# Cross-attention with token queries: moving one subtraction, writing out SyncE's order, and moving the output's 64 rows

## The chip, the cores and the metric

The kernel runs on one core of a Trainium2 chip. A core has five engines that run their own instruction queues and wait for each other through semaphores: TensorE (PE, matrix products, with its weight loads listed apart as PEld), VectorE (DVE), ScalarE (ACT), GpSimd (POOL), and SyncE (SP), which here only issues transfers (DMA). The metric is the time of one execution on the device in microseconds. Before the change: 973.11 us, the median of three runs (971.55 to 974.76).

## The reference

For each of 16 batches there are 100 query rows of width 640 and 718 encoder rows of width 384, with 4 more token rows behind them. Everything is fp32. Eight heads of width 80. Cut to what is computed:

```python
query = x @ Wq
hs = mha(query, enc @ Wk, enc @ Wv)          # over 718 encoder rows
ca_q1 = (ca^T @ Wq_ca)[:, indices]           # 100 rows out of 384, from the 4 token rows
ca_hs1 = mha(ca_q1, x, x)                    # over the 100 rows of x
ca_hs2 = mha(ca_hs1 @ Wq, ca @ Wk_ca, ca @ Wv_ca)   # over the 4 tokens
out = (hs + ca_hs2) @ Wout + b_out + x
```

## The kernel before

The encoder rows of a batch are taken as three thirds of 240 (width `KT`), each as two pieces of up to 120 keys (`KN`). V and most of K are computed with a scheme of 15 products in place of 18: sums and differences of blocks of the encoder (`enc_sums`, L466 to L485, on GpSimd, into the tile `enc`) are multiplied with sums and differences of weight blocks. A product adds into a running PSUM bank, named A to E in `V_PLAN` (L93) and `K_PLAN` (L111), and after each product the state of its bank is read out into the result: the first time by a ScalarE copy (L392), later by an addition on VectorE (L390). The next product into the same bank has to wait until the read is done. `vv.go(n)` does the next n products of V for batch b, `kk.go(n)` those of K for batch b + 1. A fifth chunk of the keys is computed plainly by `last_keys` (L543, copied out by ScalarE at L554).

The main loop goes over the batches (L1090). In a middle batch (the branch at L1183) TensorE does, in this order: the scores of batch b (L598), the small products of the second attention, the products of V for b and of K for b + 1 mixed, `last_keys`, the output projection of finished rows (`last.project`, L926), the queries of the next two batches in every second batch (L519), and the attention product of batch b (L1267, `a_ps`). VectorE meanwhile takes the maximum of the scores (`larger`, `Maximum`), and then three times `subtract` (L1112) takes it off one of three score tiles `st` of 120 x 1600; ScalarE's `exponential` (L1120) follows each. The attention product needs all three tiles.

The output has 1600 rows, cut into tiles `OC` (L33) of 128 rows, one of 64 rows and a last one of 128. A tile is projected in the iteration after the batch that completes it; in iterations 1, 5, 10 and 14 there is none. The 64 rows are completed in batch 14 and projected in the last iteration by `project_few` (L948): their two halves of 320 columns are put on the two halves of the partitions. `Last.load` (L872) brings the rows of `x` into `xn` and adds the bias on GpSimd (L883).

Orders: TensorE, VectorE, ScalarE and GpSimd follow the program's order from L1083 on (`tc.manual_schedule`). SyncE is not in that set, so its transfers are put in an order by a scheduler. They are: `xT` (L201), `enc` (L217), `rest` (L226), `mb` (L686), `ca` (L711), `xn` (L882), `out` (L942, L946, L965). A transfer at the head of SyncE's queue that waits for its buffer holds up all behind it. The tile `rest` holds two blocks of the encoder and has one buffer, read last by `last_keys` of its batch; `enc` has two buffers, read last by the products of V. `va_d` to `vb` is a transfer of 1000 KB that GpSimd issues itself (L802).

As the schedule puts them before the change, `mb` for two batches ahead stands in front of the `enc` and `rest` of the next-but-one batch.

Of the kernel before, what the change touches and what calls it, by code (L numbers as in the profile page):

```python
# [14 lines left out]
B, S, H = 16, 100, 640  # L15
# [17 lines left out]
OC = [(r, P) for r in range(0, B * S - P - 64, P)] + [(B * S - P - 64, 64), (B * S - P, P)]  # L33
# [91 lines left out]
def kernel(  # L125
# [33 lines left out]
    def pair(name):  # L159
        tile = ps2.tile([P, 2, 512], F32, tag="ps2", name=name)  # L160
        return tile
# [4 lines left out]
    def psumk(name):  # L166
        return psk.tile([P, 512], F32, tag="psk", name=name)
# [38 lines left out]
    def enc_tile(name):  # L206

        return inp.tile([P, NF, KT], F32, tag="enc", name=name)

    def rest_tile(name):  # L210
        return main.tile([P, len(A_REST), KT], F32, tag="rest", name=name)

    def load_enc(b):
        enc = enc_tile(f"enc_{b}"), None
        for u, lo, hi in ((0, 0, 3), (1, 1, 3), (2, 0, 2)):
            at = A_RAW[u, lo]
            nc.sync.dma_start(  # L217
                out=enc[0][:, at : at + hi - lo],
                in_=enct[b][:, lo:hi, u * (KT - 1) : u * (KT - 1) + KT],
            )  # L220
        return enc

    def load_rest(b, enc):
        rest = rest_tile(f"rest_{b}")
        for (u, c), i in A_REST.items():
            nc.sync.dma_start(  # L226
                out=rest[:, i], in_=enct[b][:, c, u * (KT - 1) : u * (KT - 1) + KT]
            )
        return enc[0], rest
# [634 lines left out]
    class Last:  # L864
# [51 lines left out]
        def project(self, chunks=range(HC)):  # L916
            for r, xn in self.xn.items():
                lo, n = OC[r]
                if n <= 64:
                    self.project_few(r, xn)  # L920
                    continue
                if chunks[0] == 0:
                    self.o_ps = pair(f"o_ps_{r}")
                o_ps = self.o_ps
                for c, k in [(c, k) for k in range(2) for c in chunks]:
                    nc.tensor.matmul(  # L926
                        o_ps[:n, k, : H // 2],
                        hsTs[r][:, c, :n],
                        wout_sb[:, c, k * (H // 2) : (k + 1) * (H // 2)],
                        start=(c == 0),  # L930
                        stop=(c == HC - 1),
                    )
                if chunks[-1] < HC - 1:
                    continue
                o_v = out.rearrange("b s n -> (b s) n")[lo : lo + n]
                if self.split:
                    for k in range(2):
                        cols = slice(k * (H // 2), (k + 1) * (H // 2))
                        nc.vector.tensor_tensor(
                            xn[:n, cols], o_ps[:n, k, : H // 2], xn[:n, cols], ALU.add  # L940
                        )
                        nc.sync.dma_start(out=o_v[:, cols], in_=xn[:n, cols])  # L942
                    continue
                both = xn[:n].rearrange("p (k d) -> p k d", k=2)
                nc.vector.tensor_tensor(both, o_ps[:n, :, : H // 2], both, ALU.add)
                nc.sync.dma_start(out=o_v, in_=xn[:n])  # L946

        def project_few(self, r, xn):  # L948
            lo, n = OC[r]
            o_ps = pair(f"o_ps_{r}")[:, 0]  # L950
            for c in range(HC):
                for at, cols in self.parts(n):
                    nc.tensor.matmul(
                        o_ps[at : at + n, : H // 2],
                        hsTs[r][:, c, :n],
                        wout_sb[:, c, cols],
                        start=(c == 0),
                        stop=(c == HC - 1),
                    )
            nc.vector.tensor_tensor(  # L960
                xn[:, : H // 2], o_ps[:, : H // 2], xn[:, : H // 2], ALU.add
            )
            o_v = out.rearrange("b s n -> (b s) n")[lo : lo + n]
            for at, cols in self.parts(n):
                nc.sync.dma_start(out=o_v[:, cols], in_=xn[at : at + n, : H // 2])  # L965
# [111 lines left out]
    for n in range(HC):  # L1077
# [4 lines left out]
    last, enc_next, second_next = None, load_rest(1, load_enc(1)), Second(1, xT)  # L1082
# [2 lines left out]
        mybir.EngineType.PE,  # L1085
        mybir.EngineType.DVE,
        mybir.EngineType.Activation,
    }
    ctx.enter_context(tc.manual_schedule(engines=engines))
    for b in range(B):  # L1090
# [5 lines left out]
        def loads():  # L1096

            if b == 0:
                nc.sync.dma_start(
                    out=wout_sb, in_=wout.rearrange("(c p) n -> p c n", p=P)  # L1100
                )
            if b + 2 >= B:
                return None, None, None
            x_next = xT_at[0] if b % 2 else load_x(p + 1)
            xT_at[0] = x_next
            return Second(b + 2, x_next), load_enc(b + 2), load_m(b + 2)
# [4 lines left out]
        def subtract(i):  # L1111
            return nc.vector.tensor_tensor(  # L1112
                st[i],
                st[i],
                top.over[:KN].unsqueeze(1).to_broadcast([KN, 2, ROWS]),
                ALU.subtract,
            )

        def exponential(i):
            nc.scalar.activation(st[i], st[i], AF.Exp, scale=SCALE)  # L1120
# [31 lines left out]
        if b + 1 < B:  # L1152
            kk = Keys(b + 1, enc)

        if b == 0:
            now.scores2()
            now.softmax3()
            second.scores1()
            top.go(3)
            kk.go(3)  # L1160
            top.go(1)
            first_values(3, e_in, (act, act), (0,), bank)
            kk.go(2)
            top.go()
            first_values(3, e_in, (act, act), (1,), bank)
            kk.go(3)
            first_values(0, e_in, (act, act), (0,), bank)
            kk.go(2)
            subtract(0)
            exponential(0)  # L1170
            first_values(0, e_in, (act, act), (1,), bank)
            kk.go(2)
            subtract(1)
            kk.go(3)
            exponential(1)
            second_next, enc_next, m_next = loads()
            last_keys(b + 1, enc)
            subtract(2)
            exponential(2)
            now.values2()  # L1180
            second.load()
            second.softmax1(4)
        elif b + 1 < B:  # L1183
            last.transpose()
            vv = Values(b, e_in)

            def both(n):
                vv.go(n)
                kk.go(n)

            second.scores1(seen)
            last.load()
            top.go(3)
            both(3)
            now.scores2()
            top.go(1)
            both(2)
            top.go()
            both(2)
            both(1)  # L1200
            now.softmax3()
            now.values2()
            vv.go(2)
            kk.go(1)
            subtract(0)
            exponential(0)
            both(2)
            vv.go(1)
            kk.go(2)
            both(1)  # L1210
            both(1)
            second.load()
            second_next, enc_next, m_next = loads()
            subtract(1)
            exponential(1)
            last_keys(b + 1, enc)
            subtract(2)
            exponential(2)
            second.softmax1()
            last.project()  # L1220
        else:
            room = enc_tile("spare").rearrange("p f k -> p (f k)")
            spare.extend(room[:, i * H : (i + 1) * H] for i in range(2))
            last.transpose()
            vv = Values(b, e_in)
            last.load()
            mine.load()
            top.go(3)
            vv.go(3)
            now.scores2()  # L1230
            top.go(1)
            vv.go(2)
            top.go()
            vv.go(3)
            now.softmax3()
            now.values2()
            vv.go(2)
            subtract(0)
            exponential(0)
            vv.go(5)  # L1240
            for i in (1, 2):
                subtract(i)
                exponential(i)
            last.project()
        if b + 2 < B:
            enc_next = load_rest(b + 2, enc_next)
            keys(m_next)
            enc_sums(enc_next)
        if b % 2 and b + 1 < B:
# [40 lines left out]
        last = mine  # L1290
# [55 lines left out]
```

## Time and profile before

| | |
|---|---|
| median of three runs | 973.11 us |
| the profiled execution | 972.35 us |
| its span, first to last instruction | 970.6 us |
| TensorE's mean granted clock | 0.993 of full speed |
| sums of the encoder on GpSimd (L485), 180 in all | 138.6 us |
| subtractions on VectorE (L1112), 48 | 106.2 us |
| exponentials on ScalarE (L1120), 48 | 74.0 us |
| products of the output, 128 rows (L926), 240 | 432 ns each |

The page's first part gives each engine's busy time and its share of the span. A list of waits says for whom an engine's next instruction waited, in total, how often, and the longest. The timeline lists instructions by start, with the idle time ahead of the first in brackets and what ended it. The profile shows one execution; "issue" is a gap for which it shows no cause.

### The profile page before, as it was taken

To read this page: it belongs to the slowest core of one execution; us is meant where nothing else is said; L and a number is where in the kernel's file an instruction comes from. 1 tells how busy PE (TensorE), PEld (TensorE's weight loads), DVE (VectorE), ACT (ScalarE), POOL (GpSimd) and SP (SyncE) were. 2 spreads that over 40 slices of the span, in tenths; PEclk is the share of its full clock that TensorE was granted. 3 is DMA by queue.
4 is the path that set the end of the run, shared out by engine and by line. 5 is a ranking of instruction groups with operands and counts; after the bars stand their busy time and mean duration, and the time that the engine had idled before them with its cause. 6 is when DMAs were issued, how large, how long until landed. Compare 5 with 4: busy or idle time off the path is not lost.

```text
span 970.6 us, 25628 instructions
## 1 busy us (share of the span) xinstructions
PE 942.7 (97%) x11215; PEld 803.1 (83%) x11215; DVE 674.4 (69%) x1083; ACT 359.5 (37%) x596; POOL 627.4 (65%) x572
## 2 busy tenths in 40 slices
PE   8898879999999999999999999999999999999998
PEld 5797868988788888978889887897879888897866
DVE  1358769586856868587874868668784877838783
ACT  1134424433334343342534334343432534324341
POOL 4269877594963758487673958638694576737522
PEclk9999999999999999999999999999999999999999
DMA  7840213113030211213031030301103030300101
GB/s 244 286 146 23 66 34 92 32 25 103 8 119 24 71 58 28 73 29 120 9 105 38 8 121 8 119 24 49 52 29 99 8 102 17 85 27 1 58 1 35
DMA packets 45255, 62.48 MB, mean 64 GB/s; under 512 B 13336, under 2 KB 37208, under 8 KB 43544
## 3 DMA queue, kind: packets, MB, share of 16 engines
q1 hardware_dynamic: 41608, 42.97, 14.9%
q0 software_dynamic: 2512, 16.72, 5.5%
q8 instruction: 88, 1.44, 0.6%
q10 hardware_dynamic: 1024, 1.15, 0.4%
q14 instruction: 23, 0.19, 0.1%
HBM read 55.26 MB, written 5.57 MB: 63 GB/s over the span
## 4 chain that ended last, share of the span: by engine, by line
PE 81%; POOL 7%; DMA 4%; DVE 3%; SPq 2%; ACT 1%; issue 1%; ACTq 0%; DVEq 0%; POOLq 0%
PE a_ps L1267 11%; PE s_ps L598 10%; PE v_psA L419 9%; PE v_psB L419 8%; PE k_psA L450 7%; PE o_ps L926 7%; PE q_ps L519 6%; PE k_psB L450 6%; PE kT_ps L543 5%; PE v_psC L419 3%; PE k_psC L450 2%; POOL enc L485 2%; PE v_psE L419 1%; POOL e L756 1%; PE y_ps L721 1%; PE v_psD L419 1%
## 5 line engine op out<-in xcount | busy, mean ns | idle before, releaser
L756 POOL TENSOR_TENSOR e<-ca,g 100x800 f32<-100x800 f32 x64 | 99.4, 1563 | 147.5 <-DVE most L1124 131.9
L845 POOL TENSOR_TENSOR hs<-vb,p 100x640 f32<-100x640 f32 x64 | 105.6, 1660 | 43.9 <-DVE p L831 41.3
L1267 PEld LDWEIGHTS a_ps<-vs,st 120*64 120x64 f32 (+3 forms) x3072 | 112.4, 127 | 11.1 <-ACT st L1120 5.9
L1267 PE MATMUL a_ps<-vs,st 120*64 120x81 f32 (+3 forms) x3072 | 115.6, 237 | 5.4 <-ACT st L1120 5.4
L419 PE MATMUL v_psA<-wv_sb,enc 128*120 128x320 f32 x360 | 112.1, 434 | 1.5 <-DVE vs L390 1.5
L1112 DVE TENSOR_TENSOR st<-st,over 120x1600 f32<-120x1600 f32 x48 | 106.2, 2236 | 0.0
L485 POOL TENSOR_TENSOR enc<-enc 128x240 f32<-128x240 f32 x135 | 98.6, 745 | 7.1
L485 POOL TENSOR_TENSOR enc<-enc,rest 128x240 f32<-128x240 f32 x45 | 40.0, 888 | 95.6 <-DMA rest<-in_enct 82.0
L598 PE MATMUL s_ps<-qp,kT 32*120 32x100 f32 x3072 | 97.4, 263 | 0.0
L598 PEld LDWEIGHTS s_ps<-qp,kT 32*120 32x120 f32 x3072 | 94.7, 179 | 1.6 <-issue 0.2
L763 POOL TENSOR_TENSOR e<-e,e 100x800 f32<-100x800 f32 x48 | 93.3, 1943 | 3.8
L450 PE MATMUL k_psA<-enc,wk_sb 128*128 128x240 f32 x360 | 88.8, 370 | 6.2 <-POOL enc L485 3.4
L419 PE MATMUL v_psB<-wv_sb,enc 128*120 128x320 f32 x300 | 93.1, 433 | 0.0
L615 ACT COPY st<-s_ps 120x800 f32<-120x800 f32 x64 | 49.7, 829 | 114.8 <-PE s_ps L598 114.8
L450 PEld LDWEIGHTS k_psA<-enc,wk_sb 128*128 128x128 f32 x360 | 68.6, 191 | 24.0 <-POOL enc L485 3.9
L419 PEld LDWEIGHTS v_psA<-wv_sb,enc 128*120 128x120 f32 x360 | 64.5, 183 | 24.7 <-DVE vs L390 2.7
L1124 DVE TENSOR_TENSOR most<-most,st 120x800 f32<-120x800 f32 x64 | 65.5, 1023 | 23.0 <-ACT st L609 21.9
L1120 ACT ACTIVATE st<-st 120x1600 f32<-120x1600 f32 x48 | 74.0, 1542 | 17.9 <-DVE st L1112 17.9
L852 POOL TENSOR_TENSOR hs<-hs,hs 100x640 f32<-100x640 f32 x48 | 77.1, 1607 | 3.8
L450 PE MATMUL k_psB<-enc,wk_sb 128*128 128x240 f32 x300 | 73.9, 369 | 0.0
L1278 DVE RECIPROCAL rs<-a_ps 100x4 f32<-100x4 f32 x32 | 5.8, 182 | 97.7 <-PE a_ps L1267 97.6
L419 PEld LDWEIGHTS v_psB<-wv_sb,enc 128*120 128x120 f32 x300 | 54.8, 183 | 22.3 <-DVE vs L390 0.5
(138 smaller groups left out, 1791.5 us busy)
## 6 DMA issues: line engine op xcount, KB each, us to landing
vb<-va_d POOLq DMA_DIRECT2D x16, 1000.0 KB, 5.9
enc<-in_enct SPq DMA_DIRECT2D x30, 240.0 KB, 3.8
enc<-in_enct SPq DMA_DIRECT2D x15, 360.0 KB, 3.7
xT<-in_xt SPq DMA_DIRECT2D x8, 500.0 KB, 3.5
rest<-in_enct SPq DMA_DIRECT2D x31, 120.0 KB, 3.6
xn<-in_x SPq DMA_DIRECT2D x11, 320.0 KB
out<-xn SPq DMA_DIRECT2D x11, 320.0 KB, 2.5
ca<-in_cas SPq DMA_DIRECT2D x16, 156.2 KB
```

The costliest lines, as they stand in the source:

```text
L419: nc.tensor.matmul(at[0][j][:KN, : H // 2], a_form(self.enc, f)[:, j * KN : (j + 1) * KN], wv_sb[:, W_AT[f]], start=first, stop=last, skip ...
L450: nc.tensor.matmul(at[:, i * KT : (i + 1) * KT], wk_sb[:, W_AT[f], i], a_form(self.enc, f), start=(first and i == 0), stop=last, skip_grou ...
L485: nc.gpsimd.tensor_tensor(out, left, right, op)
L598: nc.tensor.matmul(s_ps[r][:n, 256 * a + lo : 256 * a + hi], kT[rows, c, u, j * KN : (j + 1) * KN], rhs, start=(a == 0 and c == 0), stop=( ...
L756: first = nc.gpsimd.tensor_tensor(to, self.ca[:, t, :].unsqueeze(1).to_broadcast([S, NH, S]), g[:, :, t].unsqueeze(2).to_broadcast([S, NH, ...
L763: nc.gpsimd.tensor_tensor(e, e, to, ALU.add)
L845: first = nc.gpsimd.tensor_tensor(to, vb[:S, t, :].rearrange("p (h d) -> p h d", h=NH), p2[:, :, t].unsqueeze(2).to_broadcast([S, NH, D]), ...
L852: nc.gpsimd.tensor_tensor(sums, sums, to, ALU.add)
L926: nc.tensor.matmul(o_ps[:n, k, : H // 2], hsTs[r][:, c, :n], wout_sb[:, c, k * (H // 2) : (k + 1) * (H // 2)], start=(c == 0), stop=(c == ...
L1112: return nc.vector.tensor_tensor(st[i], st[i], top.over[:KN].unsqueeze(1).to_broadcast([KN, 2, ROWS]), ALU.subtract,)
L1120: nc.scalar.activation(st[i], st[i], AF.Exp, scale=SCALE)
L1267: nc.tensor.matmul(a_v[lo:hi, h % 4], st[i // 2][: KEYS[i], i % 2, h * S + lo : h * S + hi], block(i, h // 4)[: KEYS[i], h % 4], start=(i ...
```

## The change

Four things are done.

- `subtract(1)` and its exponential move forward: out of the place behind the last reads of V and K, into the middle of V's products, between the two products of V and ahead of K's. TensorE's order does not change in these batches. On VectorE the subtraction now stands between the reads of V's bank C and V's bank B.
- SyncE joins the engines that follow the program's order. With that, each batch issues, in this order: `xn` for the output, `xT` (every second batch), `ca`, `enc` of two batches on, its `mb`, then its `rest`, then `out`.
- `load_rest` moves ahead of `second.softmax1` and `last.project` for the middle batches, so that it stands before `out` in SyncE's order.
- The 64 rows of the output are projected in the last iteration after the third product of V instead of behind the projection of 128 rows. `project_few` takes its tile of `x` out of the list itself, and its PSUM bank from another pool (`psumk` instead of a pair of banks). Their transfer to the output comes ahead of that of the 128 rows.

```diff
@@ project
             for r, xn in self.xn.items():
                 lo, n = OC[r]
-                if n <= 64:
-                    self.project_few(r, xn)
-                    continue
...
-        def project_few(self, r, xn):
+        def project_few(self, r):
             lo, n = OC[r]
-            o_ps = pair(f"o_ps_{r}")[:, 0]
+            xn = self.xn.pop(r)
+            o_ps = psumk(f"o_ps_{r}")
...
         mybir.EngineType.Activation,
+        mybir.EngineType.SP,
     }
...
             kk.go(1)
             subtract(0)
             exponential(0)
-            both(2)
+            vv.go(1)
+            subtract(1)
+            vv.go(1)
+            kk.go(2)
+            exponential(1)
             vv.go(1)
             kk.go(2)
             both(1)
             both(1)
             second.load()
             second_next, enc_next, m_next = loads()
-            subtract(1)
-            exponential(1)
+            subtract(2)
             last_keys(b + 1, enc)
-            subtract(2)
             exponential(2)
+            if b + 2 < B:
+                enc_next = load_rest(b + 2, enc_next)
             second.softmax1()
             last.project()
...
             vv.go(3)
+            last.project_few(len(OC) - 2)
             now.scores2()
...
         if b + 2 < B:
-            enc_next = load_rest(b + 2, enc_next)
+            if b == 0:
+                enc_next = load_rest(b + 2, enc_next)
             keys(m_next)
             enc_sums(enc_next)
```

## The prediction

> **What bounds the kernel now.** I read the shares of the page first, then who waited for whom on TensorE, then the timelines of the stretches in which TensorE waited.
>
> ```profile
> PE 942.7 (97%) x11215; PEld 803.1 (83%) x11215; DVE 674.4 (69%) x1083; ACT 359.5 (37%) x596; POOL 627.4 (65%) x572
> ...
> PE a_ps L1267 <- ACT st L1120: 5.4, 3, 1.9
> PE k_psA L450 <- POOL enc L485: 3.4, 1, 3.4
> PE z_ps L783 <- issue: 3.2, 1, 3.2
> PE v_psA L419 <- DVE vs L390: 1.5, 1, 1.5
> ```
>
> The second block is TensorE's list of waits (total us, times, longest). TensorE is the bound: 942.7 of 970.6 us busy, so 27.9 us of gaps are all that a reordering can win, plus time at a lower clock. From 240 to 660 us it is busy throughout. The places that the change can reach: batch 1 (about 120 to 136 us), two batches in which no output projection stands before the attention product (10 and 14), and the last batch.
>
> Batch 1, from the timeline (start, length, engine):
>
> ```profile
> 118.05 0.38 SPq L686 DMA_DIRECT2D mb<-m_d  x1
> 118.52 3.61 SPq L217 DMA_DIRECT2D enc<-in_enct  x3
> 122.22 0.89 SPq L226 DMA_DIRECT2D rest<-in_enct  x2
> 126.09 1.40 POOL L485 TENSOR_TENSOR enc<-enc,rest 128x240 f32<-128x240 f32 x1 [8.07 <-DMA rest<-in_enct]
> 123.20 0.39 PE L783 MATMUL z_ps<-y,e 100*32 100x33 f32 x23 [3.18 <-issue]
> 131.81 1.97 PE L450 MATMUL k_psA<-enc,wk_sb 128*128 128x240 f32 x4 [3.41 <-POOL enc L485]
> ```
>
> SyncE takes its transfers in order. The load of `mb` for a later batch stands in front and waits for GpSimd's L696, which ends at 118.02; batch 2's `enc` and `rest` stand behind it. GpSimd waits 8.07 us for `rest`, its sums L485 come late, and TensorE waits 3.41 us for them.
>
> A wait costs more than its length. The windows (columns: TensorE, weight loads, DVE, ACT, POOL busy, then the granted clock):
>
> ```profile
> 101.13:104.54 3.41, 1.58 (x28) 1.11 (x28) 1.64 (x2) 2.36 (x3) 3.41 (x2) 1.00 0.20 47
> 104.54:107.96 3.42, 3.42 (x58) 3.42 (x55) 3.25 (x9) 0.00 (x0) 3.34 (x3) 0.50 0.00 0
> 131.85:135.26 3.41, 3.41 (x9) 2.90 (x10) 0.00 (x0) 0.56 (x1) 3.25 (x5) 0.50 0.00 0
> 677.98:681.39 3.41, 1.77 (x48) 1.61 (x48) 3.23 (x10) 2.22 (x3) 0.58 (x3) 1.00 0.59 139
> 681.39:684.80 3.41, 3.41 (x103) 3.41 (x100) 3.28 (x5) 0.03 (x1) 0.00 (x0) 1.00 0.88 293
> 906.68:910.09 3.41, 1.47 (x32) 1.14 (x32) 3.33 (x5) 2.36 (x3) 3.26 (x3) 1.00 0.39 135
> 910.09:913.50 3.41, 3.41 (x58) 3.41 (x55) 3.24 (x9) 0.00 (x0) 1.08 (x1) 0.50 0.00 0
> ```
>
> Where TensorE was busy 1.58 or 1.47 of 3.41 us, the next window ran at half clock and lost 1.71 us; at 1.77 it did not.
>
> DVE in batch 3, which repeats to 0.01 us in nearly every batch:
>
> ```profile
> 257.41 1.82 DVE L1112 TENSOR_TENSOR st<-st,over 120x1600 f32<-120x1600 f32 x1
> 257.57 4.02 POOL L845 TENSOR_TENSOR hs<-vb,p 100x640 f32<-100x640 f32 x2 [0.67 <-DVE p L831]
> 259.78 1.03 DVE L390 TENSOR_TENSOR vs<-v_psC,vs 120x320 f32<-120x320 f32 x2 [0.55 <-PE v_psC L419]
> 261.39 0.82 DVE L390 TENSOR_TENSOR vs<-v_psB,vs 120x640 f32<-120x640 f32 x1 [0.59 <-PE v_psB L419]
> 263.08 0.66 DVE L390 TENSOR_TENSOR kT<-k_psC,kT 128x480 f32<-128x480 f32 x1 [0.86 <-PE k_psC L450]
> 264.70 0.97 PE L450 MATMUL k_psC<-enc,wk_sb 128*128 128x240 f32 x4
> 268.17 4.56 DVE L1112 TENSOR_TENSOR st<-st,over 120x1600 f32<-120x1600 f32 x2
> ```
>
> DVE has gaps between the reads, and the second product into bank C of K (264.70) may only start once the first is read.
>
> **What the Trainium skill says.** "TensorE: Matmul & The Clock Gate", part 1 (the HAM clock gate): a free-running window of 3413 ns, and half rate after an idle one. The windows above agree in length and in the 0.50; here 54% idle was enough and 48% was not. "SBUF — State Buffer", section on who interferes with whom: a VectorE instruction with two SBUF inputs and a GpSimd instruction that reads SBUF lock each other out for whole instructions. The trace agrees: at 257.41 the first of GpSimd's two multiplies takes 2.79 us instead of 1.27, and at 268.17 the first subtraction takes 2.68 us instead of 1.82, since GpSimd's addition runs to 269.16. "Runtime: NRT & Kernel Launch", instruction fetch mechanics: instructions come in 16 KiB blocks over DMA. From 116.2 to 120.5 us the queue of instructions moved nothing while `vb` had 70.9% of the engines, and one block came right after; so I read the 3.18 us "issue" gap as a late fetch.
>
> **The change, part by part.** The sum is made on the profiled execution: span 970.6, 972.35 us in all, 0.76 below the median of the runs.
>
> 1. SyncE's order, batch 1. In the new order `enc` of batch 2 has no `mb` in front that waits for GpSimd; it can go once batch 0's last V product is done (93.7), and `rest` after the last read of its buffer (101.7). Both land before 106 by the 3.6 us median to landing. GpSimd goes from L696 into L485 at about 118.1 instead of 126.09, its seventh sum (5.67 us later before) is ready at 123.8, and TensorE wants it at 128.40: the 3.41 us and the half-clock window (1.71) go, 5.1 us. `xn` also no longer stands in front of batch 1's load at 56.76, which may start GpSimd's chain some 1 us sooner and with it `vb`, and shorten the fetch gap by 0 to 2 us. What is late next is DVE. GpSimd's sums now run beside L1124 and L506 on DVE; in batch 10, where they overlapped, pairs of L1124 took 2.58 and 2.39 instead of 2.0. So about 1.5 us later there, plus the bank wait of part 2, which is larger in batch 1: the gap from subtraction to second product there is 5.77 us instead of 7.09. I estimate 4.0 us net; ends 2.0 and 7.5. In later batches `enc` and `rest` also come up to 5 us earlier, but TensorE doesn't wait there: nothing. `mb` now comes behind `enc` in its own batch (about 273.5 in batch 3, needed by L696 at 269.7); L485 waits for `rest` until about 276.7 anyway.
>
> 2. Second subtraction, batches 2 to 14. Issued after the read of V's bank C (S+3.3, S being the first subtraction's start) it meets GpSimd's second multiply, which ends at S+4.18. By the pair at 268.17 it ends 1.68 us after GpSimd lets go: S+5.86. Behind it stand the read of V's bank B (0.8) and of K's bank C (0.66): S+7.24, and 0.05 to reach TensorE. TensorE's weight load for the second product came at S+7.09, the product at S+7.29. So it is 0.2 late on the load, and a product whose load was held takes 0.11 more (1.08 against 0.97): 0.12 us a batch, 0.35 in batch 11 (S+6.86). 12 x 0.12 + 0.35 = 1.8 us lost. Ends: 0, if GpSimd is not in the way, and 4. Every other read has caught up by S+9.
>
> 3. What it wins. The last exponential in ScalarE's queue stands behind the two copies of the last keys (677.95, 0.82 us), which wait for TensorE. In batch 10 it started straight after these, so the subtraction was hidden and its 1.64 us gap stays. In batch 14 the two subtractions ran to 907.9 against GpSimd's bias additions and ended 0.20 us after the copies; now only one is left. The gap becomes as in batch 10, 1.94 to 1.63, which is 48% of a window, so the half clock goes too: 0.3 + 1.7 = 2.0 us; lower end 0.3. Batch 10's 0.28 us wait for DVE may also go: 0.2.
>
> 4. The 64 rows. Twenty products of 0.135 us (2.7 in all) leave the place ahead of the last attention product and enter after V's third product. There 1.52 us of waiting for DVE (at 932.64) is filled; DVE's queue gets one addition of 0.49 ahead of that chain, so V ends some 0.4 later. The attention product could start 2.3 earlier, at 950.7, but its third score tile is ready only when the exponential that ended at 951.13 does, now 0.4 later. So it is reached at 951.7 instead of 953.5: 1.8 us won; ends 0.5 and 2.6. One output bank moves to the K pool, which is free there (no K in the last batch).
>
> Sum: 4.0 - 1.8 + 2.0 + 0.2 + 1.8 = 6.2 us. 972.35 - 6.2 = 966.15, and 0.76 on top for the median: 966.9 us.
>
> **Rivals.**
> - All early loads pay and bank C never holds: 7.0 + 2.0 + 0.2 + 1.8 = 11.0, so 962.1. For it: in batch 1 the fetch gap is large, and the hold is only 0.12. Against it: DVE's chain in batch 1 has nearly no slack.
> - Given back: batch 1 held by DVE (1.5 won), the hold 0.3 a batch (4 lost), 2.0, 0.2 and 0.5 elsewhere: 972.9, no change that can be told.
> - Slower: the subtraction loses the lock to GpSimd twice, so that the addition L852 (1.55 + 0.08) runs first as well. Then bank C is read 1.63 us later in each of 13 batches: 21.2 us, 988.1. It decides from 6.2 / 13 = 0.48 us a batch more than assumed. Against it: at 268.17 one wait was all.
>
> **How the numbers follow.** Likeliest case 0.60 (962.5 to 971), full gain 0.18, given back 0.14, slower 0.08. A measurement can tell about 0.3%, 2.9 us: 970.2 and 976.0. Faster: 0.57 of the likeliest, all of the full gain and 0.03 of the third, 0.78. Within: 0.14. Slower: 0.08. Range 961 to 972.5, which leaves out the slower case and half the edge of the second.
>
> **What would show it.** No wait of k_psA for POOL at L450 and no half-clock window after it; `enc` issued near 94 us; L1112 in two places a batch, the second 2.5 us long; a wait of 0.1 to 0.2 us on k_psC for DVE in each batch; full clock after batch 14's wait; products of 64 rows near V's third product. Waits of over 0.5 us on k_psC in each batch would make me wrong on the slow side; none at all, and no fetch gap, on the fast side.

## The result, and the profile after

The kernel after takes 963.50 us (median of four runs, 961.77 to 964.32), the kernel before, run beside it, 973.25. The ratio is 0.9898, with a 95% interval of 0.9876 to 0.9920: about 1% faster. The profiled execution of the kernel after took 964.32 us with a span of 962.6, so profile against profile 8.0 us are gone, and this execution was the slowest of its four.

The page's first part for the kernel after:

```profile
PE 941.2 (98%) x11215; PEld 799.9 (83%) x11215; DVE 673.1 (70%) x1083; ACT 359.1 (37%) x596; POOL 632.9 (66%) x572
```

TensorE's list of waits for the kernel after (us in total, times, longest):

```profile
PE a_ps L1272 <- ACT st L1119: 4.9, 3, 1.6
PE v_psA L419 <- DVE wv_sb L506: 2.6, 1, 2.6
...
PE s_ps L598 <- issue: 0.7, 1, 0.7
```

The wait of `k_psA` for GpSimd is gone, and so are the gap in `z_ps` and the wait of `v_psA` for its bank in the last batch. New are a wait of `v_psA` for the late weight sums on VectorE, and a gap in `s_ps` for which no releaser is shown.

To see where the time went, I take the first product of each score and attention stage in the two traces and compare the distances (us):

| stretch | before | after | difference |
|---|---|---|---|
| start to first scores | 66.62 | 67.62 | +1.00 |
| batch 0, scores to scores | 45.57 | 43.50 | -2.07 |
| batch 1, scores to attention | 58.68 | 54.45 | -4.23 |
| batches 2 to 9, attention to attention | 458.59 | 458.79 | +0.20 |
| from there to the attention of batch 10 | 48.38 | 48.46 | +0.08 |
| attention of batch 10 to attention of batch 11 | 64.63 | 65.57 | +0.94 |
| to the attention of batch 14 | 164.38 | 164.45 | +0.07 |
| attention of batch 14 | 10.69 | 8.75 | -1.94 |
| last batch, scores to the end | 53.11 | 51.03 | -2.08 |

The sum is -8.03. Batch 1, SyncE's queue in the kernel after (timeline: start, length of the stretch of issues, count):

```profile
59.08 37.18 SPq L217 DMA_DIRECT2D enc<-in_enct  x6
96.30 0.47 SPq L686 DMA_DIRECT2D mb<-m_d  x1
102.51 0.82 SPq L226 DMA_DIRECT2D rest<-in_enct  x2
```

`enc` of batch 2 now stands ahead of every `mb` that waits, and `rest` is issued at 102.51 instead of 122.22. What then happens on the engines in batch 1:

```profile
117.90 2.64 DVE L1123 TENSOR_TENSOR most<-most,st 120x800 f32<-120x800 f32 x2 [0.89 <-ACT st L609]
120.46 4.57 DVE L506 TENSOR_TENSOR wv_sb<-wv_sb 128x320 f32<-128x320 f32 x5
...
119.00 0.68 POOL L485 TENSOR_TENSOR enc<-enc,rest 128x240 f32<-128x240 f32 x1
...
123.38 2.46 PE L419 MATMUL v_psA<-wv_sb,enc 128*120 128x320 f32 x4 [2.63 <-DVE wv_sb L506]
```

GpSimd starts its sums at 119.00, 7 us earlier, and now they lie beside VectorE's L1123 and L506. TensorE, which needs the sums of L506 for `v_psA`, waits 2.63 us. The five weight sums now take 4.57 us. In the kernel before they took 2.21:

```profile
120.90 2.21 DVE L506 TENSOR_TENSOR wv_sb<-wv_sb 128x320 f32<-128x320 f32 x5
```

The middle batches, batch 3 of the kernel after:

```profile
252.14 1.82 DVE L1111 TENSOR_TENSOR st<-st,over 120x1600 f32<-120x1600 f32 x1
255.46 2.54 DVE L1111 TENSOR_TENSOR st<-st,over 120x1600 f32<-120x1600 f32 x1
257.92 0.81 DVE L390 TENSOR_TENSOR vs<-v_psB,vs 120x640 f32<-120x640 f32 x1
258.65 0.64 DVE L390 TENSOR_TENSOR kT<-k_psC,kT 128x480 f32<-128x480 f32 x1
...
256.39 3.01 POOL L852 TENSOR_TENSOR hs<-hs,hs 100x640 f32<-100x640 f32 x1
...
259.43 0.99 PE L450 MATMUL k_psC<-enc,wk_sb 128*128 128x240 f32 x4
```

With S for the start of the first subtraction, 252.14, the second ends at S+5.86 (255.46 + 2.54 - 252.14). Behind it two reads follow without a gap. The second, of bank C, ends at S+7.15, and the second product into bank C starts at S+7.29, as before. GpSimd's addition L852, which met the subtraction, takes 3.01 us instead of 1.55.

### The profile page after: what moved, and what is told of

Its sections match the earlier page's. It is cut to its first block, busy times and chain, and to the rows that moved or that the text cites. A ratio compares the mean times of both kernels' runs of the same rounds, so it can differ in the third digit from the quotient of the medians.

```text
span 962.6 us, 25608 instructions
## 1 busy us (share of the span) xinstructions
PE 941.2 (98%) x11215; PEld 799.9 (83%) x11215; DVE 673.1 (70%) x1083; ACT 359.1 (37%) x596; POOL 632.9 (66%) x572
## 4 chain that ended last, share of the span: by engine, by line
PE 93%; DVE 2%; SPq 2%; DMA 2%; ACT 1%; issue 1%; ACTq 0%; DVEq 0%
PE s_ps L598 12%; PE a_ps L1272 11%; PE v_psA L419 10%; PE v_psB L419 8%; PE kT_ps L543 8%; PE k_psA L450 7%; PE q_ps L519 7%; PE o_ps L923 7%; PE k_psB L450 6%; PE v_psC L419 3%; PE k_psC L450 3%; PE v_psD L419 2%; PE v_psE L419 2%; PE y_ps L721 2%; PE k_psE L450 1%; SPq L288 1%
## 5 line engine op out<-in xcount | busy, mean ns | idle before, releaser
L1272 PEld LDWEIGHTS a_ps<-vs,st 120*64 120x64 f32 (+3 forms) x3072 | 109.1, 125 | 10.9 <-ACT st L1119 5.4
L852 POOL TENSOR_TENSOR hs<-hs,hs 100x640 f32<-100x640 f32 x48 | 115.3, 2402 | 3.8
L1272 PE MATMUL a_ps<-vs,st 120*64 120x81 f32 (+3 forms) x3072 | 112.5, 234 | 4.9 <-ACT st L1119 4.9
L485 POOL TENSOR_TENSOR enc<-enc 128x240 f32<-128x240 f32 x135 | 103.9, 784 | 7.1
L1123 DVE TENSOR_TENSOR most<-most,st 120x800 f32<-120x800 f32 x64 | 65.6, 1025 | 22.3 <-ACT st L609 21.2
L485 POOL TENSOR_TENSOR enc<-enc,rest 128x240 f32<-128x240 f32 x45 | 34.7, 772 | 57.9 <-DMA rest<-in_enct 22.7
```

What stands on the lines that cost most here:

```text
L485: nc.gpsimd.tensor_tensor(out, left, right, op)
L852: nc.gpsimd.tensor_tensor(sums, sums, to, ALU.add)
L1272: nc.tensor.matmul(a_v[lo:hi, h % 4], st[i // 2][: KEYS[i], i % 2, h * S + lo : h * S + hi], block(i, h // 4)[: KEYS[i], h % 4], start=(i ...
```

## The experiments

The first three each make one part of the change to the kernel before, so that their times can be added. All others are edits of the kernel after.

**SyncE's order alone.**

```diff
+        mybir.EngineType.SP,
...
             exponential(2)
+            if b + 2 < B:
+                enc_next = load_rest(b + 2, enc_next)
             second.softmax1()
```

> Only SyncE's order and the earlier place of load_rest, on the kernel before. Theory A (from the two traces: the parts add up): batch 1 brings 4 to 5 us, batch 10 gives back about 0.9 through late instructions, nothing else moves: 4 us won, 969.3 us (968.5 to 970). In the trace: enc of batch 2 is issued before 97 us, the wait of k_psA for POOL is gone, and v_psA waits some 2.6 us for the weight sums L506 on DVE in batch 1. Theory B (the parts interact: the lead of GpSimd only pays because the second subtraction also moved): under 2 us won, over 971.3 us, with a wait of 1.5 us or more left at k_psA in batch 1.

Measured: 965.76 us, ratio 0.9949 (0.9934 to 0.9964), about 5.0 us won. Batch 1 took 54.45 us, the very length of the kernel after, with the wait of 2.66 us for L506. So batch 1's gain is that of the order alone and the second subtraction has no part in it: theory A.

Here batch 1 had no half-clock window, while the kernel after has one (123.01 to 126.42), and both take 54.45 us. Without it TensorE waits for VectorE twice more, 0.49 us at `v_psB` and 0.65 at `k_psE`. So in batch 1 VectorE's work sets the time, and that one window costs nothing.

The 0.9 us of loss that theory A expected in batch 10 shows only in part. The scores behind batch 10 took 7.72 us instead of 7.28, but a wait of 0.28 us for VectorE later in the stretch is gone, so that the stretch took 64.54 us, against 64.63 before.

**The second subtraction alone.**

```diff
             exponential(0)
-            both(2)
+            vv.go(1)
+            subtract(1)
+            vv.go(1)
+            kk.go(2)
+            exponential(1)
...
-            subtract(1)
-            exponential(1)
+            subtract(2)
             last_keys(b + 1, enc)
-            subtract(2)
             exponential(2)
```

> Only the second subtraction (with the third ahead of the last keys), on the kernel before. Theory A: the second read of bank C is hidden, the loss is 0.025 us in each of 12 batches (0.3 in all), and batch 14 brings 1.9: about 1.6 us won, 971.6 us; stage by stage the distance to the kernel before grows by under 0.05 us a batch. Theory B (as the prediction had it): 0.12 us lost in each batch and 0.35 in batch 11, 2.2 won in batches 10 and 14: 0.4 won, 972.8 us. A distance that grows by over 0.1 us a batch decides for B.

Measured: 972.32 us, ratio 1.0005 (0.9994 to 1.0016): no change that can be told. The trace agrees with theory A on the middle batches: 458.82 us for batches 2 to 9 against 458.59, which is 0.03 a batch. It also has batch 14's 8.75. Yet the 1.6 us did not show in the time, which came out nearer to theory B's number. The next run gives a reason.

**The 64 rows alone.**

```diff
             vv.go(3)
+            last.project_few(len(OC) - 2)
             now.scores2()
```

> Only the 64 rows of the output, on the kernel before. Theory A: the last attention product starts 1.8 to 2.1 us earlier and the end moves with it: 2.0 us won, 971.2 us. Theory B (the third score tile or the reads of V's banks hold the last attention product wherever the 64 rows stand): under 0.5 us won, 972.8 us or more.

Measured: 969.55 us, ratio 0.9982 (0.9969 to 0.9995), 1.75 us won. In the trace the last batch takes 51.03 us, as in the kernel after: theory A.

This run also shows something about batch 14, which it does not touch. It still waits 1.95 us there, but the attention of batch 14 took 9.06 us and not 10.69: no half clock followed. The windows of this run (TensorE, weight loads, DVE, ACT, POOL busy, then the granted clock):

```profile
906.42:909.84 3.42, 1.71 (x21) 1.20 (x20) 3.39 (x3) 2.69 (x4) 3.35 (x3) 1.00 0.73 213
909.84:913.25 3.41, 3.17 (x90) 3.18 (x92) 3.23 (x10) 0.18 (x1) 1.76 (x2) 1.00 0.04 18
```

The gap runs from 908.13 to 910.08 and reaches 0.24 us over the edge of the window; in the kernel before it lay wholly inside one, and ended 0.52 us ahead of its edge. Here the next window stays at full clock. In the run with SyncE's order alone a wait of 1.93 us, which reached 0.34 us over an edge, was not followed by half clock either (9.04 us). The Trainium skill ("TensorE: Matmul & The Clock Gate", part 1) says that the window runs free and so its effect varies from run to run. So of the 1.94 us that batch 14 shows between the two profiles, 0.3 belong to the shorter wait, and 1.64 to where the window happened to lie in the one execution profiled of before.

**One `mb` earlier in SyncE's order.** The edit makes `mb` of batch 2 stand ahead of its own `enc`.

```diff
+            if b == 0:
+                m_first = load_m(b + 2)
+                return Second(b + 2, x_next), load_enc(b + 2), m_first
             return Second(b + 2, x_next), load_enc(b + 2), load_m(b + 2)
```

> The kernel after with one transfer put back: in batch 0, mb of batch 2 stands ahead of enc again in SyncE's order. Theory A (enc and rest are held by mb, which waits for GpSimd's L696 to 118 us; this alone makes batch 1 late): enc of batch 2 is issued after 118 us, k_psA waits 3 us or more for POOL in batch 1, an issue gap of about 3 us comes back in z_ps, and the kernel is 4 to 5 us slower than the kernel after, 968 us. Theory B (what counted was xn and load_rest no longer standing in front of other transfers): within 1 us of the kernel after.

Measured: 962.88 us, ratio 0.9925 (0.9908 to 0.9943), with batch 1 at 54.44 us. Theory A's effect did not come, because I had put back the wrong transfer. This `mb` was out at 45 us. The tile has two buffers, so those of batches 2 and 3 go at once. It is the one of batch 4 that has to wait for L696. The run says nothing for theory B. It was repeated with the right one:

**`mb` of batch 4 ahead of `enc` of batch 2.**

```diff
+    xT_at, ahead = [None], {}
...
+            if b == 0:
+                ahead[2], ahead[3] = load_m(2), load_m(3)
+                return Second(b + 2, x_next), None, ahead[2]
+            m_new = ahead[b + 2] if b < 3 else load_m(b + 2)
...
-            if b == 0:
-                enc_next = load_rest(b + 2, enc_next)
             keys(m_next)
+            if b == 0:
+                ahead[4] = load_m(4)
+                enc_next = load_rest(b + 2, load_enc(b + 2))
             enc_sums(enc_next)
```

> The kernel after, with one part of SyncE's old order put back in the first batches: mb of batches 2 and 3 early, and mb of batch 4 ahead of enc and rest of batch 2, as in the kernel before. Theory A (that mb waits for GpSimd's L696 to about 118 us and holds enc and rest; this alone cost batch 1 its time): enc is issued after 118 us, k_psA waits for POOL (with what an issue gap in z_ps covers, 5 us or more together), and the stretch of batch 1 from the first score product to the attention product goes from 54.45 back to 58.7 us: 4.2 us slower than the kernel after, 967.7 us. Theory B (it was the other moves of SyncE's order): the stretch stays under 55.5 us.

Measured: 969.14 us, ratio 0.9965 (0.9949 to 0.9981). From its timeline:

```profile
117.77 0.37 SPq L686 DMA_DIRECT2D mb<-m_d  x1
118.24 3.73 SPq L217 DMA_DIRECT2D enc<-in_enct  x3
...
126.50 0.70 POOL L485 TENSOR_TENSOR enc<-enc,rest 128x240 f32<-128x240 f32 x1 [8.76 <-DMA rest<-in_enct]
...
122.86 0.39 PE L783 MATMUL z_ps<-y,e 100*32 100x33 f32 x23 [3.12 <-issue]
131.52 1.90 PE L450 MATMUL k_psA<-enc,wk_sb 128*128 128x240 f32 x4 [3.46 <-POOL enc L485]
```

Batch 1 is back at 58.79 us (58.68 before), with every mark of before: one transfer at the head of a queue is enough to undo the whole gain of batch 1. The gap in `z_ps` and the wait of `k_psA` are not two costs. In the run with the 64 rows alone, which keeps the old order, there was no gap, and `k_psA` waited 7.53 us. GpSimd's sum set the time in both cases, and the gap only covered part of the wait for it. That execution had two half-clock windows behind the wait, and its batch 1 took 61.06 us, although the edit does not touch it. With the old order, then, batch 1 is not the same from one execution to the next, and the 4.2 us hold for the profiled ones.

**The second subtraction one place later.**

```diff
-            vv.go(1)
-            subtract(1)
-            vv.go(1)
+            vv.go(2)
+            subtract(1)
             kk.go(2)
             exponential(1)
```

> The kernel after, with the second subtraction one place later on VectorE: behind the read of V's bank B, straight ahead of the read of K's bank C. Theory A (the second product into bank C has some 0.1 us to spare after the change and waits for every further delay of the read): the subtraction meets GpSimd's addition, bank C is read at S+8.2 instead of S+7.16, and each of 13 batches loses about 1 us: 13 us slower than the kernel after, 976 us, with waits of k_psC for DVE of about 1 us each. Theory B (the read of bank C has far more room, so where the subtraction stands doesn't matter): within 1 us of the kernel after.

Measured: 976.62 us, ratio 1.0046 (1.0031 to 1.0060), 13 us slower than the kernel after: theory A. Batch 3 from its timeline, in which S is 253.14:

```profile
257.12 0.82 DVE L390 TENSOR_TENSOR vs<-v_psB,vs 120x640 f32<-120x640 f32 x1 [0.58 <-PE v_psB L419]
257.87 2.76 DVE L1111 TENSOR_TENSOR st<-st,over 120x1600 f32<-120x1600 f32 x1
260.55 0.65 DVE L390 TENSOR_TENSOR kT<-k_psC,kT 128x480 f32<-128x480 f32 x1
...
261.25 1.08 PE L450 MATMUL k_psC<-enc,wk_sb 128*128 128x240 f32 x4 [0.65 <-DVE kT L390]
```

The read of bank C ends at S+8.06, 0.91 us later than in the kernel after, and each of most batches costs 0.90 us more. The reason is that in the kernel after the weight load of that product already waits for the read: it comes right behind it, at S+7.21, where it came at S+7.09 before the change. From there on every delay is paid in full.

**The late weight sums in batch 0.**

```diff
-        if b == 1:
-            weight_sums(nc.vector, wv_sb, True)
...
             subtract(2)
             exponential(2)
+            weight_sums(nc.vector, wv_sb, True)
             now.values2()
```

> The kernel after, with the five late weight sums (L506) moved on VectorE from batch 1 to the end of batch 0, behind the third exponential's subtraction. Theory A (in batch 1 VectorE has become the limit: v_psA waits 2.63 us for these sums, which GpSimd's own sums stretch to 4.57): the wait goes, k_psA finds its seventh sum within 0.5 us, and batch 1 from its first score product to its attention product shrinks by 2.6 us, or 4.3 where a half-clock window followed the wait: 960 us. Theory B (GpSimd's sums hold batch 1 anyway and VectorE's wait only covers that): k_psA waits 1.5 us or more for POOL instead, and under 1.2 us is won.

Measured: 967.42 us, ratio 0.9952 (0.9936 to 0.9968): slower than the kernel after, and neither theory's picture. Its timeline:

```profile
100.78 8.36 DVE L506 TENSOR_TENSOR wv_sb<-wv_sb 128x320 f32<-128x320 f32 x5
...
114.94 0.42 PE L598 MATMUL s_ps<-qp,kT 32*120 32x100 f32 x2 [3.25 <-DVE hs L1284]
117.69 1.69 PE L598 MATMUL s_ps<-qp,kT 32*120 32x100 f32 x25 [2.34 <-DVE hs L1284]
```

The wait for L506 in batch 1 was gone, but beside GpSimd's long additions and products the five sums took 8.36 us, the reads of the attention product stood behind them on VectorE, and TensorE waited 5.6 us for the banks.

**The late weight sums ahead of the first maximum in batch 1.**

```diff
+        if b == 1:
+            weight_sums(nc.vector, wv_sb, True)
         nc.vector.tensor_tensor(most[:KN], st[0][:, 0], st[0][:, 1], ALU.max)
...
-        if b == 1:
-            weight_sums(nc.vector, wv_sb, True)
```

> The kernel after, with the five late weight sums (L506) still in batch 1 on VectorE but ahead of the first maximum of the scores (L1138) instead of behind the second, so beside GpSimd's five short instructions L696. Theory A (the wait of v_psA comes from the place of these sums in VectorE's queue): they end before 120.7 us, the wait of 2.63 us falls under 0.5, no more than 1 us of it comes back at k_psA for POOL, and the stretch from the first score product of batch 1 to its attention product, 54.45 us in the kernel after, shrinks by 1.6 to 4.3 us: about 960.5 us. Theory B (as in the earlier place in batch 0, GpSimd's lock stretches them and everything behind them on VectorE): the stretch stays or grows, and a new wait for DVE of over 2 us shows in batch 1.

Measured: 963.98 us, ratio 0.9915 (0.9897 to 0.9933), batch 1 at 54.40 us, as in the kernel after. Both theories miss:

```profile
114.45 2.73 DVE L506 TENSOR_TENSOR wv_sb<-wv_sb 128x320 f32<-128x320 f32 x5
...
114.04 4.34 POOL L696 TENSOR_TENSOR m<-mb,hmask 128x64 f32<-128x64 f32 x5
...
126.35 1.08 PE L450 MATMUL k_psA<-enc,wk_sb 128*128 128x240 f32 x4 [3.02 <-POOL enc L485]
```

VectorE's sums are done at 117.2 and nobody waits for them. In their place L696 takes 4.34 us instead of 3.41, GpSimd's sums end later, and `k_psA` waits 3.02 us for them. So putting one engine first makes the other late, as if both worked through one budget of time. This fits what the Trainium skill says ("SBUF — State Buffer", who interferes with whom) of an exclusive lock between the two; that the total is what counts was not tried by taking any of the work away.

**One transfer of `vb` left out.**

```diff
-            second.load()
+            if b == 10:
+                second.vb = now.vb
+            else:
+                second.load()
```

> The kernel after, with one transfer of vb (1000 KB, issued in batch 10 for batch 11) left out; batch 11 uses the old tile. Theory A (instruction blocks come late where vb shares the DMA engines with SyncE's transfers, and the second subtraction pushed vb back into that time): the gaps of TensorE in s_ps and z_ps at about 683 and 690 us (0.74 and some 0.4) and GpSimd's gap of 5 us at 680 go, and the stretch from the attention product of batch 10 to that of batch 11 shrinks by 1.2 us: 962.3 us. Theory B (the gaps have another cause, such as GpSimd's lock or reads of PSUM): they stay, and the time does too.

Measured: 962.12 us, ratio 0.9902 (0.9885 to 0.9920). Batch 10 to 11 took 64.10 us instead of 65.57. First the kernel after, then this run (timelines):

```profile
671.81 0.59 POOL L802 DMA_DIRECT2D vb<-va_d  x1
...
680.28 0.69 POOL L485 TENSOR_TENSOR enc<-enc,rest 128x240 f32<-128x240 f32 x1 [5.05 <-issue]
...
682.98 0.78 PE L598 MATMUL s_ps<-qp,kT 32*120 32x100 f32 x19 [0.74 <-issue]
...
690.04 1.03 PE L783 MATMUL z_ps<-y,e 100*32 100x33 f32 x64
```

```profile
678.10 0.69 POOL L485 TENSOR_TENSOR enc<-enc,rest 128x240 f32<-128x240 f32 x1 [0.47 <-issue]
...
691.24 0.75 PE L783 MATMUL z_ps<-y,e 100*32 100x33 f32 x64
```

Without the 1000 KB, GpSimd's gap falls from 5.05 to 0.47 us, TensorE's gap is gone and `z_ps` takes 0.75 us again: theory A, in that this transfer causes the gaps.

What comes late behind it is not the same for both engines, as the packets in the traces show. For GpSimd it is data. Its first sum reads `rest`, whose landing the trace of the kernel after lacks, so that the gap says "issue". But the last packet of `rest` ended at 679.58 there, 0.70 us ahead of the sum; in the kernel before, whose gap names `rest`, that distance is 0.69. Without `vb` the last packet ended at 677.61.

For TensorE it is instructions. Its "issue" gaps of over 0.2 us behind the start-up are 14 in all traces together, the 3.18 us of batch 1 before among them. Each ends 1.29 to 1.66 us after a packet of 16 KB on a queue of instructions has ended. In batch 10 that packet ended 8.70 us after the start of the attention product in the kernel after, 6.67 before, and 5.69 without `vb`. This agrees with the Trainium skill ("Runtime: NRT & Kernel Launch", instruction fetch mechanics), where instructions are fetched over DMA, but not with its remark that this is hidden.

In the run with SyncE's order alone `vb` went out at 666.87, 3.9 us ahead of the attention product, and the list of waits has no gap. In the kernel after it goes 1.0 us ahead of it, because two of GpSimd's additions had waited 1.5 us each for the subtractions. With the second subtraction alone `vb` also goes 1.0 us ahead, and the scores behind batch 10 took 0.53 us longer than before the change; with the order alone, 0.44 longer; with both, 1.18, and `z_ps` 0.28 more. So each of the two parts costs about half a microsecond there by itself, and together they cost more than the sum.

**The third exponential ahead of the copies of the last keys.**

```diff
-            last_keys(b + 1, enc)
             exponential(2)
+            last_keys(b + 1, enc)
```

> The kernel after, with the third exponential ahead of the two copies of the last keys on ScalarE, in batches 1 to 14. Theory A (in batches 10 and 14 the exponential's data are ready at 670.5 us and it waits only behind the copies, which wait for TensorE): the waits of a_ps for ACT of 1.64 us in batches 10 and 14 go, the other batches stay: 3.2 us faster than the kernel after, 960.3 us. Theory B (the third subtraction is what the exponential waits for): the waits stay above 1 us and the time stays within 0.8 us.

Measured: 961.83 us, ratio 0.9890 (0.9875 to 0.9905). TensorE's list of waits of this run:

```profile
PE a_ps L1272 <- ACT st L1119: 1.6, 1, 1.6
...
PE s_ps L598 <- issue: 1.3, 1, 1.3
```

Of three waits of `a_ps` one is left; the attention products of batches 10 and 14 take 6.90 us instead of 8.75, which is 3.7 us: theory A for the mechanism. The time shows less. The profiled execution had two half-clock windows in batch 1 (55.83 us instead of 54.45), and the gap in `s_ps` grew. The interval overlaps that of the kernel after, so whether this version beats it in time stays open.

**Both together,** with the second subtraction as in the change, and (below) without it:

```diff
+        if b == 1:
+            weight_sums(nc.vector, wv_sb, True)
         nc.vector.tensor_tensor(most[:KN], st[0][:, 0], st[0][:, 1], ALU.max)
...
-        if b == 1:
-            weight_sums(nc.vector, wv_sb, True)
...
-            last_keys(b + 1, enc)
             exponential(2)
+            last_keys(b + 1, enc)
```

> The kernel after, with the weight sums ahead of the first maximum in batch 1 and the third exponential ahead of the copies of the last keys in batches 1 to 14. Theory A (the two waits are independent and add up): 2.6 us from batch 1 and 3.3 from batches 10 and 14, less 0.5 for a longer instruction gap in batch 10: 5.4 us faster than the kernel after, 958 us. Theory B (another wait takes the place of each): over 961 us.

> As the run before, but with the second subtraction left in its old place: SyncE's order, the 64 rows, the weight sums ahead of the first maximum, and the second and third subtraction and exponential ahead of the last keys. Theory A (the second subtraction's move costs 0.025 us a batch and, by pushing vb back, the instruction gaps in batch 10; its only gain was at the wait of batch 14, which the new order of ScalarE takes away anyhow): no instruction gap in batch 10, a wait of a_ps for ACT of 0.3 to 0.8 us in batches 10 and 14: 957.5 us, 0 to 1 us faster than the run before. Theory B (two subtractions ahead of the attention product are too late for it): waits of over 1.2 us in batches 10 and 14, and slower than the run before by 1 us or more.

Measured: 963.56 us, ratio 0.9907 (0.9889 to 0.9926), and 966.00 us, ratio 0.9933 (0.9916 to 0.9950). The first keeps the 6.90 us of batches 10 and 14, but batch 1 has the wait of 3.03 us for GpSimd, now with a half-clock window behind it. This is theory B, for batch 1. The second also has that wait. It waits 0.46 us in batch 10 but still 1.92 in batch 14, which is theory A for batch 10 and theory B for batch 14. And it does have a gap of 0.82 us in `s_ps`, against theory A, although `vb` went out 3.9 us ahead of the attention product: the lead of `vb` is not the whole of the matter. The packet of instructions came late there too, and the gap ended 1.49 us behind it. The attention product of batch 14 took 6.90 us in the first and 9.04 in the second. So with the exponential put first, the second subtraction's move is worth something in the trace; the intervals of the two times overlap.

## Why the prediction was right

The forecast was 966.9 us, the result 963.50, inside the range of 961 to 972.5, and faster as the likeliest case had it. By its own steps:

1. **SyncE's order, batch 1: 4.0 forecast, 4.23 measured** between the profiles; 4.23 also with the order alone, and 4.34 when the one transfer is put back. The mechanism was right, and so was that VectorE is late next. The terms were off in ways that cancel. VectorE's delay was put at 1.5 us and some bank wait, and TensorE waits 3.80 for it in the run with the order alone (2.66, 0.49 and 0.65), where no half-clock window hides a part. On the other side I valued the gap in `z_ps` at 0 to 2 us of its own. It was cover for the wait for GpSimd, 6.6 us in all with it, not 3.41. That the sum came within 0.2 us is luck, the more so since batch 1 of the old order took 61.06 us in another execution.

2. **The hold of K's bank C: 1.8 lost forecast, 0.3 measured** (0.20 in batches 2 to 9, some 0.03 a batch). The meeting with GpSimd was forecast to the hundredth (S+5.86). The term that failed is what follows. My S+7.24 is not the sum of the numbers beside it (5.86, 0.8 and 0.66 make 7.32), and both are too late. Instructions in a row on VectorE start before the one ahead has ended: the read of bank B at S+5.78, 0.08 us before the end of the subtraction, and the two reads 0.73 us apart for 0.81 us of length. So bank C was free at S+7.15. The load came 0.12 us later than before and the product on time. The extra 0.35 in batch 11 showed with the subtraction alone (0.42 over two products), not in the kernel after (0.03).

3. **Batches 14 and 10: 2.0 and 0.2 won forecast.** Batch 14 shows 1.94, but 1.64 of it is a half-clock window that other executions with the same wait do not have. To count it in full was the weak step. In all traces together `a_ps` waits 29 times 1.64 us, and half clock never follows; it waits 8 times 1.82 to 1.95 us, and half clock follows 4 times. So in these traces the shorter wait rules the window out, but the longer one brings it only when enough of it falls into one window. In batch 10 VectorE's 0.28 us wait did go and brought 0.55. What I had not foreseen is the gap behind the late `vb`, which took 1.46 there (1.18 in `s_ps`, 0.28 in `z_ps`): I looked for late instructions only where the profile of before showed them.

4. **The 64 rows: 1.8 forecast, 2.08 in the trace, 1.75 in the time of the part alone.** From the timeline of the kernel after:

```profile
923.37 2.91 PE L951 MATMUL o_ps<-wout_sb,hsT 128*64 128x320 f32 x20
...
939.39 5.59 PE L923 MATMUL o_ps<-wout_sb,hsT 128*128 128x320 f32 x20
944.92 6.30 PE L1272 MATMUL a_ps<-vs,st 120*64 120x81 f32 x168
```

The rows stand in the place of the wait and the attention product follows the 128 rows without a gap, so the third score tile was not what held it. The forecast made the product wait for that tile at its start. The tile was ready 0.68 us after the start (at 945.60), and in batch 10 the product came to its gap for it only 0.77 us in.

Not in the sum: batch 0 was 2.07 us shorter. It waited 1.64 us instead of 1.83 and no half clock followed. In the run with the 64 rows alone, which leaves batch 0 as it was, this was so too (43.35 us), so it is not shown to come from the change. The start took 1.00 more; it varies from 65.24 to 68.73 us among the traces. Without these two and the half-clock window of batch 14 the two profiles are 5.3 us apart, so the 8.0 owe something to the executions. The slower rival, that the subtraction loses the lock twice, did not happen: it waited once, and then it was GpSimd's addition that waited for it (256.39, 3.01 us).

The parts alone give -5.0, +0.5 and -1.75, together -6.3 us, close to the forecast of -6.2; the whole gave -9.9 by its ratio (-7.8 to -12.1). The granted clock of the executions points to half-clock windows: its mean is 0.9915 in 35 executions of the kernel before, 0.9942 in six with the order alone and 0.9955 in the four of the kernel after. One such window takes 0.0018 of it, so by an estimate the change takes away about two, and the profile of before, at 0.993, has about one fewer than usual. With intervals of 1 to 1.5 us on each part, whether the parts help each other stays open.

## What to carry to other kernels

When a transfer is late, look first at what stands at the head of its queue and whom that waits for: here one small load kept GpSimd waiting for 8.1 us. Value a wait together with the gaps ahead of it, since a gap can be cover for the same late event, and ask before moving work between two engines that exclude each other whether the sum of their work, not the order, sets the time. Whether a wait of nearly 2 us brings a half-clock window depends on how it falls into the windows, so count the cost of one only in part, for the edit that removes the wait and for the one that adds it. And a gap without a named cause may still have one in the packets of the DMA queues.

## What the runs showed of the hardware that was not expected

- How empty a window must be. The changes of clock in all 14 traces lie on a grid of 3413 ns, so the windows between them can be laid out too, some 3800 at full clock after the start-up. Of those with TensorE busy less than 1.61 us, as the profile models it, all 26 were followed by half clock. Of those from 1.61 to 1.71 it was 3 of 6, and of all above, one. That one is in the run with the late subtraction, where the gaps of `s_ps` fell among short products:

```profile
690.00:693.42 3.42, 1.99 (x57) 1.81 (x58) 1.36 (x3) 0.00 (x0) 3.26 (x5) 1.00 0.00 1
693.42:696.83 3.41, 3.41 (x73) 3.41 (x71) 0.00 (x0) 1.34 (x2) 3.25 (x6) 0.50 0.02 5
```

- The same five VectorE instructions (L506) took 2.21, 2.73, 4.57 and 8.36 us, by what GpSimd ran beside them. In the kernel after the two engines take turns, one instruction each, and one of VectorE's lasts 0.86 to 0.99 us instead of 0.48. Beside additions and products of 1.3 to 1.5 us, in the early place in batch 0, it lasts 1.55 to 2.16. So short instructions pay most beside long ones.
- TensorE can run out of instructions while a transfer of 1000 KB is under way: its gaps without a releaser end 1.29 to 1.66 us after the end of a packet of instructions, as worked out with the run that leaves out `vb`.
